# Fixed tiles with free lists, numbered admission, and a norm written in turned order, in a four-layer transformer kernel

## The chip, the cores and the metric

The kernel runs on one core of one Trainium2 chip. The metric is the device time of one execution in microseconds (us). Before the change, three runs gave a median of 2664.83 us (2660.78 to 2669.65).

The engines have short names in the profile: PE (TensorE, matrix products; PEld is its weight load), DVE (VectorE), ACT (ScalarE), POOL (GpSimd) and SP (SyncE, which here issues all DMAs).

## What is computed

Four transformer layers act in turn on x, of 16 samples x 256 tokens x 256 features, in fp32. Attention has 16 heads of 16 features. The context has 77 tokens a sample. Cut to what matters, for one sample:

```python
# layer 0: modulated by cond; self-attention masked by blocks, rotary on q and k
x = x + g_msa * (attn(rope(norm(x) @ Wq), rope(norm(x) @ Wk), norm(x) @ Wv, mask) @ Wo)
x = x + g_x   * (attn(norm(x) @ cq_W, ctx @ ck_W, ctx @ cv_W, mask_c) @ co_W)
x = x + g_mlp * (gelu(norm(x) @ W1 + b1) @ W2 + b2)
# layer 1: cross-attention alone; layer 2: self-attention, cross-attention, MLP
# layer 3: self-attention with rotary, cross-attention with rotary, MLP
```

Each norm subtracts the mean of a token's features, divides by their standard deviation, then scales and shifts by values that a small product of the condition gives ("modulation"). The attention inside is softmax(q k / 4) v.

## The kernel before

**Blocks and stages.** The unit of work is one sample in one sublayer, a *block* (256 tokens x 256 features, two tiles of 128 tokens). All of x stays in SBUF (`x_sb`). The sublayers are named by letters, which are also the ends of the tiles' names: a (self-attention, layer 0), ac (cross), b (MLP); cx (cross, layer 1); c (self, layer 2), cc (cross), d (MLP); e (self, layer 3), ec (cross), f (MLP). There are 16 blocks of each.

**One attention block**, in `attention` from line 726:

- `norm_tasks` (line 484): DVE takes mean and variance (`norm_stats`, 465), POOL makes the factor (`rstd_of`, 473) and writes the normed x into `xn` (line 497, two instructions of 128x256). For all but the first two blocks of stage a, DVE then turns 32x32 pieces of `xn` into `y` (line 526), SP sends `y` to DRAM (`yd`, line 532) and fetches it back with features on the partitions (`xr`, line 536), and ACT applies the modulation (`xT`, line 547). The two other blocks (`direct`) are turned by PE (line 505).
- PE makes q, k and v (lines 627, 679, 799). ACT and DVE write q and k into a tile `kq`, v goes to `vt`. With rotary, DVE and POOL rotate (lines 691, 694, 699) and PE turns back (719).
- Scores for the row maxima: PE in row tiles of 32 partitions (lines 840 and 852), DVE reduces each bank (lines 866, 870, 874) into `mx`. When all of a block's maxima are there, DVE turns `mx` (line 886), and SP moves them through DRAM into `kq` (lines 889, 893), where they enter the second product.
- Scores again, with the maximum subtracted (line 937), exponentials on ACT into `e` (949, 951), values on PE in column tiles (line 960), a turn, division and turn back on DVE and POOL (969, 976, 982, 986).
- `residual` (line 998): PE multiplies by the output weights (line 1007), DVE or POOL adds to x.

An MLP block makes `h` (PE line 1050, ACT line 1055) and ends in `residual` too.

**What sets the order.** All instructions are laid out by a planner in the kernel's own text, class `Order` (line 74). Each step is a task: an engine ("NO" for steps that only take a buffer), an assumed duration, its dependencies, buffers that it takes and holds, and a priority number, smaller first. `solve` simulates the engines on the host, and each engine's program is the order in which `solve` starts the tasks. On PE, ready tasks go by (priority, number). "NO", DVE, ACT and POOL go by the time at which a task became ready, then priority (lines 179 and 180). Tasks with `rp` 0 and 1 use different halves of PE's rows and are started in pairs (`choose`, line 154).

**Buffers.** `CAPS` (line 222) says how many there are of each kind: 8 PSUM banks "b", 5 "kq", 5 "v", 3 "mx", 2 "mr", 2 "ec" (four `e` tiles each), 1 "xn", 1 "y", 2 "ts" and so on. "b", "kq" and "v" come from free lists (`FREE`, line 82). All others are rings, made by rotating tile pools: a slot comes back only when all slots taken before it are back.

**Lines.** For "mx", "mr", "e" and "av" there is besides an order of places: a block joins the lines when it is admitted (`joins`, line 747), and a task with a `line` can start only when its block is at the head (`room`, line 119). The turn of the maxima (line 894) is in line "mr".

**Admission.** A block is admitted by a "NO" task (line 745), once its x is done, and takes a "kq" and a "v". Priorities are given out in steps of 10 in the order of the loops, which `wave` (line 1063) makes: for self- and cross-attention, it puts cross block b two steps after self block b. Some steps take theirs from this numbering: the load of x for block b (line 1186), and the third modulation "m0m" (line 1191), which waits for `admitted[-8]`, the eighth of the last blocks in that order.

Of the kernel before, what the change touches and what calls it, by code (L numbers as in the profile page):

```python
# [10 lines left out]
F32 = mybir.dt.float32  # L11
# [49 lines left out]
class Task:  # L61
    __slots__ = ("eng", "dur", "run", "deps", "take", "prio", "rp", "left", "ready", "outs", "held", "start", "end", "no", "since", "kind", "joins",
                 "line", "last", "more", "lat", "first", "mb")
# [10 lines left out]
class Order:  # L74
# [7 lines left out]
    FREE = ("b", "kq", "v")  # L82

# [3 lines left out]
    def add(self, eng, dur, run, deps=(), take=(), use=(), prio=0, rp=None, kind=None, joins=(),  # L87
            line=None, last=True, more=0.0, lat=0.0, first=False, mb=0.0):


        t = Task()
        t.joins, t.line, t.last, t.more, t.lat, t.first, t.mb = joins, line, last, more, lat, first, mb
# [11 lines left out]
    def solve(self):  # L104
        import heapq
        caps = self.caps
        taken = {k: 0 for k in caps}
        done_no = {k: set() for k in caps}
        ring = {k: 0 for k in caps}
        loose = {k: list(range(caps[k])) for k in self.FREE}  # L110
# [6 lines left out]
        lines = {}  # L117

        def room(t, more=()):
            if t.line is not None and (not lines.get(t.line[0]) or lines[t.line[0]][0] != t.line[1]):  # L120
                return False
            need = {}
            for h in list(t.take) + list(more):
                need[h.tag] = need.get(h.tag, 0) + 1
            return all(len(loose[k]) >= n if k in loose else taken[k] + n <= ring[k] + caps[k]
                       for k, n in need.items())

        def begin(ts):
# [6 lines left out]
            for t in ts:  # L135
                for h in t.take:
                    h.no = loose[h.tag].pop(0) if h.tag in loose else taken[h.tag]
                    taken[h.tag] += 1
                for name, key in t.joins:
                    lines.setdefault(name, []).append(key)  # L140
                if t.line is not None and t.last:
                    lines[t.line[0]].pop(0)
# [28 lines left out]
        while n_done < len(self.tasks):  # L171
            progress = True
            while progress:
                progress = False
                for eng in list(waiting):
# [3 lines left out]
                    cand.sort(key=lambda t: (t.prio, t.no) if eng == "PE" else (not t.first, t.prio, t.no) if eng == "SP" else  # L179
# [13 lines left out]
            while events and events[0][0] <= now + 1e-9:  # L193
                _, _, t = heapq.heappop(events)
                n_done += 1
                for h in t.held:
                    h.users -= 1
                    if not h.users and h.tag in loose:
                        loose[h.tag].append(h.no)
                    elif not h.users:  # L200
                        done_no[h.tag].add(h.no)
                        while ring[h.tag] in done_no[h.tag]:
                            done_no[h.tag].discard(ring[h.tag])
                            ring[h.tag] += 1
# [9 lines left out]
def pixart_kernel(ctx: ExitStack, tc: tile.TileContext, x, cond_t, ctx_in, mask_c, mask_s, tables, vecs, rows,  # L214
# [17 lines left out]
    kqs = [const.tile([P, 2, 2, 512], F32, name=f"kq{i}") for i in range(CAPS["kq"])]  # L232
    banks = [ps.tile([P, 512], F32, name=f"bank{i}") for i in range(CAPS["b"])]

# [42 lines left out]
    mrs, vs = [], []  # L277
# [5 lines left out]
    for j in range(CAPS["v"]):  # L283
        vs.append(const.tile([P, NT, H, 32], F32, name=f"vt{j}"))
# [54 lines left out]
    def load_weights(src, block, deps=(), prio=-1):  # L339

        if len(BLOCKS[block]) == 2:
            hs, views, tasks = [Hold("kq"), Hold("kq")], {}, {}

            def run(i, name, n):
                w = kqs[hs[i].no].rearrange("p a b n -> p (a b n)")
# [30 lines left out]
    def modulation(name, src, col, shift_at, scale_at, c_t, bias, norm=None, gate=None, deps=(), prio=0, gprio=None):  # L376
# [3 lines left out]
        def load():  # L380
            s["w"] = kqs[hw.no][:, 0]
# [29 lines left out]
        def load2():  # L411
            s["wg"] = kqs[hw2.no][:, 0]
# [11 lines left out]
        def rowtake():  # L424
            d = gate_d[g_row]
            pg, g2 = s["pg"], work.tile([P, NT, D], F32, tag="tmp", bufs=CAPS["tmp"], name=f"g2_{name}")
# [23 lines left out]
    def bias_tile(name, rest, deps, prio):  # L450
# [3 lines left out]
        def mm():  # L454
            s["p"] = psum(h)
            s["t"] = work.tile([P, 1, D], F32, tag="bias", bufs=CAPS["bias"], name=f"bias_{name}")
# [8 lines left out]
    def norm_stats(src, parts, n, name, c=""):  # L465
# [611 lines left out]
    def later(prio):  # L1077
        return prio + 1000
# [306 lines left out]
```

## Time and profile before

| | us |
|---|---|
| runs, median (lowest to highest) | 2664.83 (2660.78 to 2669.65) |
| the profiled execution's own time | 2664.59 |
| its span, first to last instruction | 2662.8 |
| time around the span | 1.8 |
| stage a with its start, about | 0 to 460 |
| ac / b / cx | 460 to 638 / 862 / 1122 |
| c / cc / d | 1122 to 1459 / 1633 / 1847 |
| e / ec / f | 1847 to 2249 / 2440 / 2663 |

The stage bounds are read from where the last results of one stage end (`oT`, `h`); neighbouring stages overlap there.

How to read the rows below. In a group of instructions, "L526 DVE STREAM_TRANSPOSE y_e<-xn_e ... x16 | 17.6, 1103 | 29.9 <-..." is: line, engine, operation, output and input, count, then the time that the group was busy (us), the mean of one (ns), the idle time of the engine just before, and who ended it. fp32 products appear as two records each. In a view by windows, each row has the window, its length, then busy time and count for PE, PEld, DVE, ACT and POOL, the granted clock of PE (1.00 is full), and the DMA share. In the view of a tile, a row has the shortest, median and longest duration in ns, then the first and last start in us. The profiled chain of work that ended last follows from the last instruction back to what released each step. PE's rows overlap in time, since a record's end is modelled; starts are measured.

### The profile page before, as it was taken

To read this page: it belongs to the slowest core of one execution; us is meant where nothing else is said; L and a number is where in the kernel's file an instruction comes from. 1 tells how busy PE (TensorE), PEld (TensorE's weight loads), DVE (VectorE), ACT (ScalarE), POOL (GpSimd) and SP (SyncE) were. 2 spreads that over 40 slices of the span, in tenths; PEclk is the share of its full clock that TensorE was granted. 3 is DMA by queue.
4 is the path that set the end of the run, shared out by engine and by line. 5 is a ranking of instruction groups with operands and counts; after the bars stand their busy time and mean duration, and the time that the engine had idled before them with its cause. 6 is when DMAs were issued, how large, how long until landed. Compare 5 with 4: busy or idle time off the path is not lost.

```text
span 2662.8 us, 55746 instructions
## 1 busy us (share of the span) xinstructions
PE 2595.9 (97%) x21512; PEld 1821.4 (68%) x21512; DVE 1678.8 (63%) x4537; ACT 1250.2 (47%) x2511; POOL 1062.0 (40%) x1413
## 2 busy tenths in 40 slices
PE   8999999999999899999999999999999999998999
PEld 5556565666888666566666667888666665666888
DVE  7888887774241677777776775211888887895110
ACT  2444445664333456555555564232455555554222
POOL 4233333556452364233334556432233334556310
PEclk9999999999999899999999999999999999998999
DMA  5101111234221121111111123211000001121110
GB/s 169 30 23 33 33 31 40 65 98 129 63 80 44 51 63 56 56 35 40 43 39 35 58 77 97 68 60 44 28 30 27 27 27 37 44 73 54 56 60 28
DMA packets 159747, 143.08 MB, mean 54 GB/s; under 512 B 24648, under 2 KB 124216, under 8 KB 158712
## 3 DMA queue, kind: packets, MB, share of 16 engines
q1 hardware_dynamic: 159480, 139.51, 16.9%
q8 instruction: 169, 2.77, 0.4%
q14 instruction: 98, 0.80, 0.1%
HBM read 91.86 MB, written 47.61 MB: 52 GB/s over the span
## 4 chain that ended last, share of the span: by engine, by line
PE 87%; DVE 6%; POOL 2%; ACT 2%; DMA 1%; issue 1%; DVEq 0%; ACTq 0%; SPq 0%; POOLq 0%
PE bank L1007 19%; PE bank L937 13%; PE bank L1050 12%; PE bank L960 11%; PE bank L627 7%; PE bank L840 7%; PE bank L679 6%; PE bank L799 5%; PE bank L852 2%; PE bank L719 2%; PE bank L930 2%; DVE mx_e L870 1%; DVE mx_c L870 0%; DVE mx_ec L874 0%; PE bank L390 0%
## 5 line engine op out<-in xcount | busy, mean ns | idle before, releaser
L937 PE MATMUL bank<-kq 32*128 32x256 f32 (+1 forms) x5120 | 615.8, 397 | 2.3 <-DMA kq<-mrow 0.8
L937 PEld LDWEIGHTS bank<-kq 32*128 32x128 f32 (+1 forms) x5120 | 350.2, 168 | 171.1 <-issue 99.0
L840 PE MATMUL bank<-kq 32*128 32x512 f32 x1536 | 420.5, 642 | 1.9 <-ACT e_e L951 1.6
L951 ACT ACTIVATE e_a<-bank 128x512 f32<-128x512 f32 x256 | 138.0, 596 | 178.7 <-PE bank L840 152.4
L866 DVE CUSTOM_DVE_ANT_0 junk<-bank,ctxT_masks 128x256 f32<-128x256 f32 x448 | 188.3, 420 | 36.5 <-issue 3.6
L951 ACT ACTIVATE e_e<-bank 128x512 f32<-128x512 f32 x256 | 136.1, 598 | 140.8 <-PE bank L840 79.3
L870 DVE TENSOR_REDUCE mx_c<-bank 128x2 f32<-128x512 f32 x256 | 160.2, 680 | 37.8 <-PE bank L840 36.9
L951 ACT ACTIVATE e_c<-bank 128x512 f32<-128x512 f32 x256 | 136.1, 599 | 97.2 <-PE bank L840 54.4
L870 DVE TENSOR_REDUCE mx_e<-bank 128x2 f32<-128x512 f32 x256 | 161.3, 680 | 25.3 <-PE bank L840 24.6
L852 PE MATMUL bank<-kq 32*128 32x154 f32 x2048 | 169.7, 312 | 4.2 <-ACT kq L634 3.0
L840 PEld LDWEIGHTS bank<-kq 32*128 32x128 f32 x1536 | 128.6, 185 | 34.8 <-issue 9.0
L852 PEld LDWEIGHTS bank<-kq 32*128 32x128 f32 x2048 | 132.3, 187 | 21.1 <-issue 4.6
L1013 DVE TENSOR_TENSOR x_sb<-x_sb,bank 128x512 f32<-128x512 f32 x80 | 54.0, 675 | 126.7 <-PE bank L1007 122.3
L1050 PE MATMUL bank<-xT_b,kq 128*128 128x256 f32 x512 | 117.1, 385 | 0.0
L1055 ACT ACTIVATE h_f<-bank,vec 128x256 f32<-128x256 f32 x128 | 52.3, 466 | 136.9 <-PE bank L1050 136.0
L1055 ACT ACTIVATE h_d<-bank,vec 128x256 f32<-128x256 f32 x128 | 52.0, 466 | 135.7 <-PE bank L1050 118.4
L1050 PE MATMUL bank<-xT_f,kq 128*128 128x256 f32 x512 | 113.5, 379 | 0.0
L1007 PE MATMUL bank<-kq,h_b 128*128 128x256 f32 x512 | 113.5, 379 | 0.0
L1050 PE MATMUL bank<-xT_d,kq 128*128 128x256 f32 x512 | 113.4, 380 | 0.0
L1007 PE MATMUL bank<-kq,h_f 128*128 128x256 f32 x512 | 113.1, 379 | 0.0
L1007 PE MATMUL bank<-kq,h_d 128*128 128x256 f32 x512 | 113.1, 379 | 0.0
L1050 PEld LDWEIGHTS bank<-xT_b,kq 128*128 128x128 f32 x512 | 97.8, 193 | 13.9 <-issue 0.8
(329 smaller groups left out, 5722.5 us busy)
## 6 DMA issues: line engine op xcount, KB each, us to landing
kq<-in_mod_dram SPq DMA_DIRECT2D x10, 512.0 KB
cin<-in_ctx_in_dram SPq DMA_DIRECT2D x36, 128.0 KB
x_sb<-in_x_dram SPq DMA_DIRECT2D x16, 256.0 KB
yd<-y_ac SPq DMA_DIRECT2D x16, 256.0 KB
xr_ac<-yd SPq DMA_DIRECT2D x16, 256.0 KB
yd<-y_b SPq DMA_DIRECT2D x16, 256.0 KB
xr_b<-yd SPq DMA_DIRECT2D x16, 256.0 KB
gb_b<-gate_g0m SPq DMA_DIRECT2D x16, 256.0 KB
```

Of the source, the lines that this page charges most:

```text
L627: nc.tensor.matmul(dst[:, g, :], lhsT=w[:, k, g * P:(g + 1) * P], rhs=xT[:, k, :], start=(k == 0), stop=(k == NC - 1))
L679: nc.tensor.matmul(u["p"][0:r, at:at + D], lhsT=xT()[:, k, t * P:t * P + r], rhs=w()[:, k, :], start=(k == 0), stop=(k == NC - 1))
L799: nc.tensor.matmul(ps[0:rows_n, t * D:(t + 1) * D], lhsT=xT[:, k, t * P:t * P + rows_n], rhs=wv[kv][:, k, :], start=(k == 0), stop=(k == N ...
L840: ls.append(lambda ps=ps, R=R, keys=keys: nc.tensor.matmul(ps.rearrange("p (s k) -> p s k", k=N), lhsT=s["qx"][R, 0, g, t * P:(t + 1) * P] ...
L852: ls.append(lambda ps=ps, R=R, keys=keys, tt=tt: nc.tensor.matmul(ps[:, 2 * tt * n:2 * (tt + 1) * n].rearrange("p (s k) -> p s k", k=n), l ...
L866: nc.vector.tensor_tensor_reduce(junk, u[i][:, i2 * N:(i2 + 1) * N], mb[:, t, :], -1.0, 3.0e38, ALU.add, ALU.min, m[:, i2, g, t:t + 1])
L870: nc.vector.tensor_reduce(m[:, :, g, t], u[i].rearrange("p (s k) -> p s k", k=N), AX.X, ALU.max, negate=True)
L937: (lambda ps=u[i], R=R, q=q: nc.tensor.matmul(ps[0:rows_n, q * N:(q + 1) * N], lhsT=s["kz"][R, q, g, kc * P:kc * P + rows_n], rhs=s["qx"][ ...
L951: nc.scalar.activation(e, u[i][0:rows_n], AF.Exp)
L960: nc.tensor.matmul(u5["p"][32 * r:32 * r + 32, 1 - q, :], lhsT=s["v"][0:rows_n, kc, 8 * g + 2 * r + 1 - q, :], rhs=s["e", g, kc, r][0:rows ...
L1007: nc.tensor.matmul(u["p"][:, t, :], lhsT=lhsT(k, t), rhs=w()[:, k, :], start=(k == 0), stop=(k == nk - 1))
L1050: nc.tensor.matmul(u["p"][:, j, :], lhsT=wv["w1"][:, k, f * P:(f + 1) * P], rhs=s["xT"][:, k, :], start=(k == 0), stop=(k == NC - 1))
```

## The change

1. All SBUF buffers are made once as fixed tiles (`SHAPES`, `pools`), and `buf(hold)` gives the tile whose number the planner drew. All kinds now have free lists: a slot is back as soon as its own users are done. The counts in `CAPS` stay. The four `e` tiles of one "ec" become slices of one tile. The DRAM buffers `yd` and `mrow` go by the drawn number too.
2. `joins`, `line` and the lines are gone. The two value products of a group of heads (line 960) may run in either order; the first to run starts the sum in PSUM.
3. "NO" tasks go by priority instead of by the time at which they became ready. `wave` sorts the blocks by b plus 0, 16 or 32 for the first, second and third kind of block.
4. The norm on POOL (line 497), except in the two direct blocks, writes `xn` with the features of each half in the order (f, j) instead of (j, f): it reads x in order and writes every 32nd element. The turn on DVE (line 526) then reads runs of 32 neighbours instead of every fourth element. The planner's duration for that turn goes from 0.7 to 0.75.

The diff, cut to its core (each `work.tile` or `small.tile` elsewhere becomes `buf` of its hold in the same way):

```diff
@@ solve
-        taken = {k: 0 for k in caps}
-        done_no = {k: set() for k in caps}
-        ring = {k: 0 for k in caps}
-        loose = {k: list(range(caps[k])) for k in self.FREE}
+        loose = {k: list(range(n)) for k, n in caps.items()}
...
         def room(t, more=()):
-            if t.line is not None and (not lines.get(t.line[0]) or lines[t.line[0]][0] != t.line[1]):
-                return False
             need = {}
             for h in list(t.take) + list(more):
-                need[h.tag] = need.get(h.tag, 0) + 1
-            return all(len(loose[k]) >= n if k in loose else taken[k] + n <= ring[k] + caps[k]
-                       for k, n in need.items())
+                if h.no < 0:
+                    need[h.tag] = need.get(h.tag, 0) + 1
+            return all(len(loose[k]) >= n for k, n in need.items())
...
-                    cand.sort(key=lambda t: (t.prio, t.no) if eng == "PE" else (not t.first, t.prio, t.no) if eng == "SP" else
+                    cand.sort(key=lambda t: (t.prio, t.no) if eng == "PE" else (not t.first, t.prio, t.no) if eng in ("SP", "NO") else
                               (not t.first, t.ready - self.FAVOUR * any(h.tag == "b" for h in t.held), t.prio, t.no))
...
-                    if not h.users and h.tag in loose:
+                    if not h.users:
                         loose[h.tag].append(h.no)
-                    elif not h.users:
-                        done_no[h.tag].add(h.no)
-                        while ring[h.tag] in done_no[h.tag]:
-                            done_no[h.tag].discard(ring[h.tag])
-                            ring[h.tag] += 1
@@ norm_tasks
         def scale():
-            xn = s["xn"] = work.tile([P, NT, D], F32, tag="xn", bufs=CAPS["xn"], name=f"xn_{name}")
+            xn = s["xn"] = buf(hn)
             for t in range(NT):
-                nc.gpsimd.tensor_scalar(xn[:, t, :], x_sb[:, b, t, :], s["mv"][:, t, 0:1], s["rstd"][:, t:t + 1],
-                                        ALU.subtract, ALU.mult)
+                to, of = xn[:, t, :], x_sb[:, b, t, :]
+                if not direct:
+                    to, of = (a.rearrange(f"p (c {z}) -> p c j f", c=NC, f=4) for a, z in ((to, "f j"), (of, "j f")))
+                nc.gpsimd.tensor_scalar(to, of, s["mv"][:, t, 0:1], s["rstd"][:, t:t + 1], ALU.subtract, ALU.mult)
...
         def turn32():
-            s["y"] = work.tile([P, 4, NT * NC * 32], F32, tag="y", bufs=CAPS["y"], name=f"y_{name}")
+            s["y"] = buf(hy)
             nc.vector.transpose(s["y"].rearrange("p f (u i) -> p f u i", i=32),
-                                s["xn"].rearrange("p t (c j f) -> p f (t c) j", j=32, f=4))
+                                s["xn"].rearrange("p t (c f j) -> p f (t c) j", j=32, f=4))
@@ attention
         x_t = add("NO", 0.0, admit, deps=[x_done[b], *norm_deps],
-                  take=[h_kq, h_v], prio=prio,
-                  joins=[("mx", nm), ("mr", nm)] +
-                        [(i, (nm, g, kc)) for i in ("e", "av") for g in range(NC) for kc in range(nk)])
+                  take=[h_kq, h_v], prio=prio)
...
-        a = add("DVE", 0.2, turn, first=True, deps=red, take=[h_mr], use=[h_mx], prio=prio, line=("mr", nm))
+        a = add("DVE", 0.2, turn, first=True, deps=red, take=[h_mr], use=[h_mx], prio=prio)
@@ wave
-    def wave(kinds):
-
-        nxt = [0] * len(kinds)
-        order = []
-        step = 0
-        while any(i < B for i in nxt):
-            for j in range(len(kinds) - 1, -1, -1):
-                b = step - 2 * j
-                if 0 <= b < B:
-                    order.append((j, b))
-                    nxt[j] += 1
-            step += 1
-        return order
+    def wave(*late):
+
+        return sorted(((j, b) for j in range(len(late)) for b in range(B)), key=lambda z: (z[1] + late[z[0]], -z[0]))
@@ the loops
-    for j, b in wave([0, 1]):
+    for j, b in wave(0, 16):
...
-    for j, b in wave([0, 1, 2]):
+    for j, b in wave(0, 16, 32):
...
-    for j, b in wave([0, 1]):
+    for j, b in wave(0, 16):
```

## The prediction

> **What bounds the kernel now.** I read the page first: busy time by engine, and under it the chain that ended last.
>
> ```profile
> span 2662.8 us, 55746 instructions
> PE 2595.9 (97%) x21512; PEld 1821.4 (68%) x21512; DVE 1678.8 (63%) x4537; ACT 1250.2 (47%) x2511; POOL 1062.0 (40%) x1413
> PE 87%; DVE 6%; POOL 2%; ACT 2%; DMA 1%; issue 1%; DVEq 0%; ACTq 0%; SPq 0%; POOLq 0%
> ```
>
> PE is the bound. All its idle time is 2662.8 - 2595.9 = 66.9 us, so a change that only reorders can win no more than that, plus what it takes out of PE's busy time. The timeline of PE in a self-attention stage shows what could be taken out:
>
> ```profile
> 2055.16 0.48 PE L937 MATMUL bank<-kq 32*128 32x256 f32 x2
> ...
> 2055.92 0.38 PE L937 MATMUL bank<-kq 32*128 32x256 f32 x2
> 2056.24 1.99 PE L1007 MATMUL bank<-w_e,oT_e 128*128 128x256 f32 x8
> 2058.16 1.07 PE L960 MATMUL bank<-e_e,vt 128*32 128x256 f32 x16
> ```
>
> Where PE stays in one shape, in the MLP stages, 32 records of 128x256 take 6.91 us (the chain in order of time), 0.216 each. Here eight of them run from 2056.24 to 2058.16, 1.92 us instead of 1.73. The pair of row-tiled tasks ahead of them runs 1.08 us (2055.16 to 2056.24) where its four rounds need 0.86. So each change of tile shape costs about 0.2 us, and the order of the tasks on PE sets how many changes there are. That is the only large lever here.
>
> Then the busy times by stretch of time (us, PE, PEld, DVE, ACT, POOL). First three steady stretches, of stages a, c and e; then the four handovers between attention stages, and the end of stage ec.
>
> ```profile
> 100.00:400.00 300.00, 299.21 (x2817) 178.01 (x2812) 260.73 (x1029) 142.53 (x269) 99.65 (x129) 1.00 0.11 31
> 1150.00:1400.00 250.00, 249.85 (x2265) 156.04 (x2264) 185.71 (x380) 144.87 (x281) 85.22 (x115) 1.00 0.14 41
> 1900.00:2200.00 300.00, 297.33 (x2695) 185.79 (x2696) 251.87 (x530) 151.76 (x289) 95.57 (x132) 0.99 0.09 28
> ```
>
> ```profile
> 425.00:475.00 50.00, 47.25 (x534) 30.55 (x526) 29.56 (x88) 30.16 (x57) 21.73 (x34) 1.00 0.21 62
> 1090.00:1125.00 35.00, 32.58 (x289) 18.54 (x288) 27.81 (x63) 16.05 (x36) 12.71 (x19) 0.95 0.24 66
> 1405.00:1470.00 65.00, 61.40 (x678) 39.09 (x674) 38.77 (x107) 40.35 (x84) 34.78 (x48) 1.00 0.14 42
> 2215.00:2270.00 55.00, 50.24 (x520) 30.87 (x514) 36.40 (x115) 30.53 (x60) 25.58 (x37) 1.00 0.11 35
> 2395.00:2440.00 45.00, 37.21 (x317) 23.18 (x313) 32.58 (x93) 17.95 (x34) 39.20 (x57) 0.81 0.20 69
> ```
>
> In steady state PE is full in all three stretches, with DVE at 87%, 74% and 84%. The idle time sits at the handovers: 2.75 + 2.42 + 3.60 + 4.76 = 13.5 us.
>
> **The order of the stages does not move.** The text of the loops suggests that self- and cross-attention blocks were interleaved and now run one after the other. The trace says that they already run one after the other. The maxima of stage a and of its cross-attention ac are turned (line 886) at these times:
>
> ```profile
> L886 DVE STREAM_TRANSPOSE mt_a<-mx_a x16: 211/211/213, 50.8 to 432.2; 128x32 f32<-128x32 f32 x16
> L886 DVE STREAM_TRANSPOSE mt_ac<-mx_ac x16: 171/211/213, 432.3 to 610.5; 128x32 f32<-128x32 f32 x16
> L874 DVE TENSOR_REDUCE mx_ac<-bank x32: 429/468/480, 388.7 to 454.9; 128x4 f32<-128x308 f32 x32
> ```
>
> Admission went by readiness, all a blocks are ready early, and an ac block only when its a block is done. So the new keys (b, then 16 + b, then 32 + b) give the order that the trace has: I cost that edit at nothing in steady state. What does change is who comes first on PE at a handover. Before, the first ac blocks have smaller priority numbers than the last a blocks. The last row shows the result: the maxima of the first ac blocks start at 388.7, yet the first of their turns is at 432.3, 0.1 us after the last turn of a. They did their work early, and then stood in line "mr". Now the last a blocks go first, and nobody stands in line.
>
> **Part by part.**
>
> (1) Fixed tiles, free lists, no lines. No instruction and no DMA is added or removed, none moves to another engine. No buffer count changes. In steady state blocks pass first-in first-out anyway, so rings and lists give the same slots. I cost it at 0 there. At the handovers it can win at most the 13.5 us of PE idle; at least 0. Nearest row for what cannot be won is the drain at the end of ec, where no next block exists: 45.0 - 37.2 = 7.8 us idle. I take half, 6.8 us.
>
> (2) Steps that the new numbers move. Modulation "m0m" waits for the eighth of the last admissions, now ac block 8 instead of 11. It issues a 512 KB and a 256 KB load on SP, takes a kq buffer for each, and 16 records on PE (2.2 us where the trace has one at 873.40). The PE work is due either way; on SP it passes the row-maxima transfers of three blocks at most, and those are put first. Cover: four other kq buffers with blocks in flight. Without it, one admission would slip by one load. The loads of x for blocks 3 on also get smaller numbers and pass ten context loads on SP, which stage ac needs only from 388 us. I take 0 for both.
>
> (3) The turn on DVE (line 526) reads 16 bytes apart before, and contiguous runs of 32 after. Groups by line, mean ns after the comma:
>
> ```profile
> L526 DVE STREAM_TRANSPOSE y_e<-xn_e 128x512 f32<-128x512 f32 x16 | 17.6, 1103 | 29.9 <-DMA yd<-y_e 9.4 <-POOL x_sb L563 9.0 <-DMA yd<-y_d 9.0
> L969 DVE STREAM_TRANSPOSE ts_e<-bank 128x512 f32<-128x512 f32 x32 | 22.6, 707 | 14.1 <-PE bank L960 13.9
> L497 POOL TENSOR_SCALAR xn_e<-x_sb,mv_e,rstd_e 128x256 f32<-128x256 f32 x32 | 38.9, 1223 | 3.7 <-DVE y_e L526 1.9 <-DVE y_d L526 0.8
> L982 POOL TENSOR_TENSOR od_e<-ts_e,rec_e 128x128 f32<-128x128 f32 x64 | 24.4, 401 | 99.5 <-DVE rec_e L976 99.5
> L699 POOL TENSOR_TENSOR qk_e<-qk_e,r_qk_e 128x512 f32<-128x512 f32 x32 | 40.5, 1269 | 81.8 <-DVE r_qk_e L694 78.5 <-PE bank L719 3.4
> ```
>
> Same operation, same size, contiguous source: 0.71 us against 1.10. That source is PSUM; the turn of half the size from SBUF to SBUF (line 986, mean 429 ns) lies on the same line, so SBUF is no slower. Ends: 1.10 (no gain) and 0.70; I take 0.71. There are 10 x 16 - 2 = 158 such turns (two blocks go by PE), so DVE loses 158 x 0.39 = 61.6 us of work. How much reaches the end? DVE is 6% of the chain, 160 us of its 1679 busy: about 9.5% of DVE's time is on the path. 61.6 x 0.095 = 5.9 us. From below: 0. From above: all of it in the self stages a and e, where DVE is at 84 to 87%: (14 + 16) x 0.39 = 11.7 us. I take 5.9. In the MLP stages it is worth nothing, PE runs without a change of shape there. What is late next is PE itself.
>
> (4) The norm write on GpSimd (line 497): 316 of its 320 instructions (those of the two blocks by PE stay) now write elements 128 bytes apart, and read as before. No row has such a write. Nearest: line 982 writes runs of 16 and takes 3.1 ns an element (401/128); line 699 writes contiguously and takes 2.5 (1269/512), some of the difference being a fixed part. The norm itself takes 4.8 (1223/256). A gain is excluded, since reads are contiguous in both and writes get less so. [...] line 526 against 969 is 1.10/0.71 = 1.55. Applied to GpSimd, 1.22 becomes 1.90, 316 x 0.68 = 215 us more of its time, 40% busy becomes 48%, and with 2% of the chain (53 of 1062 us, 5%) that is +10.7 us. By the rows it is 0: even the slow turn moves an element in 1103/512 = 2.2 ns, and GpSimd spends 4.8 on each, so a write that takes that long is hidden behind its own work. I take 0 and keep +10.7 for the range.
>
> **The sum.** The profiled execution took 2664.59 us (span 2662.8 and 1.8 around it), 0.24 under the median of 2664.83. 2664.59 - 6.8 - 5.9 = 2651.9, so 2652 us, -0.5%. Against the median it is the same to the digit that matters. A difference under 0.3% (8 us, 2656.8 to 2672.8) can't be told from no change here.
>
> **The rivals.**
>
> *A, the forecast*, 2652; its own range 2639 (13.5 and 11.7 both won) to 2657. Chance 0.43.
>
> *B, it does nothing*: DVE's saved time lands in its own idle (37% of the span), and the handovers stay as they are because DMA latency and the last block's chain set them, not places. For it: the only long wait of PE that isn't the start, 7.8 us on xT_cx (line 627), is a norm chain that no part shortens by more than 0.4 us. 2660 to 2665. Chance 0.24.
>
> *C, slower by more changes of shape*. Priorities decide which task PE takes next. If the new order strings row-tiled pairs singly between other work, each extra run costs 1.08 - 0.86 = 0.21 us. One more in each of the 16 x 7 = 112 attention blocks is 23.5 us: 2664.6 - 5.9 + 23.5 = 2682. It outweighs the gains and shows as slower from about (8 + 5.9)/0.21 = 66 extra runs. For it: nothing in the planner's choice among ready tasks favours the shape that PE is in. Against: in steady state the order of readiness and place is the same. Chance 0.18, with a little from (4).
>
> *D, the same lever the other way*: as many runs fewer, as free buffers let two pairs follow each other. 2651.9 - 23.5 = 2628. For it: the cross blocks' maxima that stood in line for 40 us held mx buffers. Against: eight PSUM banks hold only two pairs. Chance 0.15.
>
> **How the numbers follow.** Faster by over 0.3%: A's 0.43 and D's 0.15, less a piece of A near the bound: 0.57. Slower: C, 0.18. Same: the rest, 0.25. The range reaches to D and to C, 2622 to 2682, which leaves out some 6% below and 8 to 10% above.
>
> **What would show it.** Line 526 at 0.71 us, x158, and DVE's busy time at 1679 - 62 = 1617 (step 3). Line 497 at 1.22 us; at 1.6 or more [...] step 4 is wrong. The first turn of ac within some 10 us of its eighth reduction, and PE idle of 7 us instead of 13.5 over the four handovers (step 1). PE busy within 10 us of 2596: A and B; 2615 or more is C, 2575 or less is D. The forecast is wrong above all if the new numbers change how PE's tasks fall together in steady state, which the trace of before can't show.

## The result, and the profile after

The changed kernel takes 2630.61 us (median of four runs, 2626.68 to 2638.0), the kernel before 2667.24 us in the same comparison (2660.78 to 2672.21). The ratio is 0.9867 (95% interval 0.9835 to 0.9899): 1.3% faster, where 0.5% was forecast. The time lies inside the range and near the figure of rival D (2628), but not by D's mechanism, as shown below.

The page's first lines for the changed kernel, and its two groups that part 4 touches (line 497 is now 491, line 526 is 519):

```profile
span 2629.7 us, 56144 instructions
PE 2575.5 (98%) x21512; PEld 1813.2 (69%) x21512; DVE 1627.7 (62%) x4537; ACT 1255.4 (48%) x2511; POOL 1113.5 (42%) x1413
...
L491 POOL TENSOR_SCALAR xn<-x_sb,mv,rstd 128x256 f32<-128x256 f32 x320 | 451.1, 1464 | 108.4 <-DVE y L519 97.8
...
L519 DVE STREAM_TRANSPOSE y<-xn 128x512 f32<-128x512 f32 x158 | 110.9, 702 | 298.9 <-DMA yd<-y 257.6
```

The same instructions do the same work (x21512, x4537, x2511, x1413); the 398 more in the first line are all semaphore waits of the sequencers. The turn went from 1.10 to 0.70 us; the norm write from 1.22 to 1.46. PE's idle time went from 66.9 to 2629.7 - 2575.5 = 54.2 us, and its busy time fell by 20.4 us.

The turns of the maxima (line 886, now 872) in the view of a line, which gives no letter of a stage any more because the tiles are shared:

```profile
L872 DVE STREAM_TRANSPOSE mr<-mx x112: 211/211/215, 51.5 to 2384.4; 128x32 f32<-128x32 f32 x112
```

From the single starts behind this row: 15th and 16th turn of stage a at 392.0 and 414.5, first turn of ac at 426.1, 1.3 us after that block's last reduction ended at 424.8. Before, that reduction ended at 394.1 and the turn came at 432.3, after 38 us in line. Most of this wait is gone because the reductions of ac now start later (414.6 instead of 388.7); the turn itself comes only 6 us earlier. The stages come in the same sequence as before.

The windows show where PE's idle time went. First the four handovers, placed at the same work as before's; then stage ec, and its last 45 us. Columns are as before: length, then PE, PEld, DVE, ACT, POOL.

```profile
422.80:472.80 50.00, 49.00 (x584) 30.77 (x580) 27.98 (x77) 30.17 (x55) 20.49 (x28) 1.00 0.17 51
1069.00:1104.00 35.00, 34.48 (x245) 23.28 (x246) 29.54 (x64) 15.40 (x32) 14.02 (x21) 1.00 0.18 56
1393.60:1458.60 65.00, 64.62 (x738) 43.07 (x735) 46.77 (x124) 41.64 (x87) 34.80 (x48) 1.00 0.17 51
2194.50:2249.50 55.00, 53.67 (x599) 35.88 (x591) 40.13 (x124) 33.82 (x66) 26.09 (x38) 1.00 0.13 39
2228.30:2414.60 186.30, 179.89 (x1810) 120.47 (x1809) 153.80 (x484) 100.56 (x197) 124.29 (x175) 0.99 0.20 64
2369.60:2414.60 45.00, 40.30 (x377) 27.97 (x370) 32.38 (x102) 23.96 (x47) 41.33 (x56) 0.96 0.26 85
```

The handovers have 1.00 + 0.52 + 0.38 + 1.33 = 3.2 us of PE idle, against 13.5. Stage ec has 186.3 - 179.9 = 6.4. The row of before for stage ec, which the prediction did not show:

```profile
2248.80:2440.00 191.20, 176.89 (x1767) 116.04 (x1768) 157.80 (x473) 95.90 (x186) 117.88 (x172) 0.96 0.19 59
```

That is 14.3 us idle and a mean clock of 0.96. The clock is a third place to look. In both traces the granted clock is either 1.00 or 0.50. Below are the longest stretches at 0.50, and the sum over all of them: before, and then after.

```profile
875.00:888.70 13.70, 5.91 (x21) 5.05 (x21) 9.28 (x12) 2.36 (x4) 10.90 (x8) 0.50 0.16 53
...
2397.30:2414.40 17.10, 12.66 (x80) 8.60 (x84) 14.04 (x38) 2.50 (x4) 14.04 (x19) 0.50 0.23 70
sum 51.20, PE 38.83 PEld 24.71 DVE 39.05 ACT 11.13 POOL 38.99; mean PE 6.47 PEld 4.12 DVE 6.51 ACT 1.86 POOL 6.50
```

```profile
876.70:886.90 10.20, 3.46 (x8) 2.84 (x9) 8.21 (x12) 1.09 (x2) 8.64 (x7) 0.50 0.16 52
...
2385.40:2388.80 3.40, 3.14 (x7) 2.01 (x7) 2.78 (x11) 1.95 (x4) 2.54 (x2) 0.50 0.26 90
sum 23.80, PE 16.80 PEld 13.00 DVE 16.39 ACT 5.61 POOL 18.64; mean PE 3.36 PEld 2.60 DVE 3.28 ACT 1.12 POOL 3.73
```

At half clock PE does about half as much. In the trace of the changed kernel, eight products of one shape take 3.61 us from their first start to the next row's start in the stretch 1607.1 to 1610.5, and 1.72 us just after it, at full clock:

```profile
1607.10 3.68 PE L992 MATMUL bank<-w_c,oT 128*128 128x256 f32 x8 [1.73 <-DVE oT L971]
1610.71 1.07 PE L945 MATMUL bank<-ec,v 77*32 77x256 f32 x16
...
1622.18 1.89 PE L992 MATMUL bank<-w_c,oT 128*128 128x256 f32 x8
1623.90 7.07 PE L992 MATMUL bank<-kq,ec 128*128 128x256 f32 x32
```

Over all neighbouring products of that shape, the median from start to start is 216 ns at 1.00 and 427 ns at 0.50, in both traces.

PE was busy for 38.8 us at half clock before, and for 16.8 after. If half of that is lost, the loss went from 19.4 to 8.4 us. So the span of 33.1 us less splits, in these two profiles, into 12.7 of idle, about 11.0 of clock (an estimate), and a rest of 9.4 in PE's busy time. That rest may be waiting inside what counts as busy, since the ends of PE's records are modelled; no view here shows it.

### The profile page after: what moved, and what is told of

It is laid out like the page before. It is cut to its first block, busy times and chain, and to the rows that moved or that the text cites. A ratio compares the mean times of both kernels' runs of the same rounds, so it can differ in the third digit from the quotient of the medians.

```text
span 2629.7 us, 56144 instructions
## 1 busy us (share of the span) xinstructions
PE 2575.5 (98%) x21512; PEld 1813.2 (69%) x21512; DVE 1627.7 (62%) x4537; ACT 1255.4 (48%) x2511; POOL 1113.5 (42%) x1413
## 5 line engine op out<-in xcount | busy, mean ns | idle before, releaser
L936 ACT ACTIVATE ec<-bank 128x512 f32<-128x512 f32 (+1 forms) x1152 | 608.5, 596 | 514.0 <-PE bank L828 260.7
L491 POOL TENSOR_SCALAR xn<-x_sb,mv,rstd 128x256 f32<-128x256 f32 x320 | 451.1, 1464 | 108.4 <-DVE y L519 97.8
L858 DVE TENSOR_REDUCE mx<-bank 128x2 f32<-128x512 f32 x544 | 341.6, 681 | 46.0 <-PE bank L828 43.7
L945 PE MATMUL bank<-ec,v 128*32 128x256 f32 (+1 forms) x5120 | 347.9, 385 | 5.8 <-ACT ec L936 3.6
L1035 PE MATMUL bank<-xT,kq 128*128 128x256 f32 x1536 | 341.4, 379 | 0.0
L992 PE MATMUL bank<-kq,ec 128*128 128x256 f32 x1536 | 339.7, 379 | 0.0
L992 PEld LDWEIGHTS bank<-kq,ec 128*128 128x128 f32 x1536 | 291.5, 190 | 39.5
L1035 PEld LDWEIGHTS bank<-xT,kq 128*128 128x128 f32 x1536 | 290.5, 190 | 40.4 <-issue 1.6
L862 DVE TENSOR_REDUCE mx<-bank 128x4 f32<-128x308 f32 x512 | 211.9, 468 | 55.4 <-PE bank L922 25.3
L854 DVE CUSTOM_DVE_ANT_0 junk<-bank,ctx 128x256 f32<-128x256 f32 x448 | 188.8, 421 | 45.2 <-PE bank L828 12.2
```

The costliest lines, as they stand in the source:

```text
L491: nc.gpsimd.tensor_scalar(to, of, s["mv"][:, t, 0:1], s["rstd"][:, t:t + 1], ALU.subtract, ALU.mult)
L854: nc.vector.tensor_tensor_reduce(junk, u[i][:, i2 * N:(i2 + 1) * N], mb[:, t, :], -1.0, 3.0e38, ALU.add, ALU.min, m[:, i2, g, t:t + 1])
L858: nc.vector.tensor_reduce(m[:, :, g, t], u[i].rearrange("p (s k) -> p s k", k=N), AX.X, ALU.max, negate=True)
L862: nc.vector.tensor_reduce(m[:, :, g].rearrange("p s t -> p t s"), u[i][:, 0:4 * n].rearrange("p (t s k) -> p t s k", s=2, k=n), AX.X, ALU. ...
L936: nc.scalar.activation(e, u[i][0:rows_n], AF.Exp)
L945: nc.tensor.matmul(u5["p"][32 * r:32 * r + 32, 1 - q, :], lhsT=s["v"][0:rows_n, kc, 8 * g + 2 * r + 1 - q, :], rhs=s["e", g, kc, r][0:rows ...
```

## The price of the half clock, from all runs

Each timed run gives its span and its mean granted clock. Since the clock is 1.00 or 0.50, the time at half clock is 2 x (1 - clock) x span, to some 5 us (the clock has three digits). Over 199 runs of the kernels below, each taken against the mean of its own kernel and batch of runs, a microsecond at half clock goes with 0.38 us more span (correlation 0.92). By the 216 and 427 ns above, about 0.5 would be the price if PE never idled in it (an estimate). So two executions of one kernel differ mostly by this term. With it taken out, kernels can be compared "at equal clock": that is an estimate (the last column), since the price was found between runs of one kernel and is carried over to differences between kernels. It is also a correlation; no run separates a price of the clock from late waits that bring both.

| kernel (runs) | ratio to before, 95% | mean span | half clock | span less 0.383 x half clock |
|---|---|---|---|---|
| before (43 / 24 / 12, by batch) | 1 | 2663.4 / 2662.4 / 2662.3 | 51.3 / 51.5 / 51.9 | 2643.8 / 2642.7 / 2642.4 |
| changed (4) | 0.9867 (0.9835 to 0.9899) | 2629.7 | 25.0 | 2620.1 |
| turn_only (22) | 0.9979 (0.9969 to 0.9989) | 2658.2 | 49.3 | 2639.3 |
| no_turn (6) | 0.9908 (0.9885 to 0.9931) | 2639.3 | 43.1 | 2622.8 |
| numbers_only (22) | 0.9999 (0.9987 to 1.0011) | 2662.7 | 64.2 | 2638.1 |
| lines_kept (6) | 0.9928 (0.9910 to 0.9946) | 2644.6 | 35.3 | 2631.1 |
| lists_only (11) | 1.0053 (1.0036 to 1.0069) | 2677.0 | 55.5 | 2655.7 |
| old_numbers (5) | 1.0416 (1.0394 to 1.0437) | 2776.3 | 156.6 | 2716.2 |
| before_lag15 (14) | 1.0009 (0.9997 to 1.0021) | 2665.6 | 52.6 | 2645.5 |
| after_lag15 (6) | 0.9891 (0.9872 to 0.9911) | 2636.4 | 31.6 | 2624.3 |
| ot_first (6) | 0.9937 (0.9918 to 0.9956) | 2644.2 | 32.6 | 2631.7 |
| lines_ot3 (7) | 0.9944 (0.9925 to 0.9964) | 2646.8 | 34.8 | 2633.5 |
| before_ot3 (6) | 0.9922 (0.9904 to 0.9939) | 2640.1 | 48.4 | 2621.6 |
| after_ot3_told (5) | 0.9866 (0.9844 to 0.9887) | 2625.6 | 58.8 | 2603.0 |

For the change itself the runs say what the two profiles said: about 26 us less at half clock, worth some 10 us by this estimate, and 23 us that remain at equal clock.

## The experiments

The theory after the result: most of the gain comes from the order (parts 1 to 3), a small part from the turn (part 4). The rivals: the turn alone; the numbers alone; luck of a greedy planner, in which any small edit could have moved the time as much.

**The turn alone, and all but the turn.** *turn_only* is the kernel before with only part 4 (without the planner's figure for it, so that the order stays):

```diff
-                nc.gpsimd.tensor_scalar(xn[:, t, :], x_sb[:, b, t, :], s["mv"][:, t, 0:1], s["rstd"][:, t:t + 1],
-                                        ALU.subtract, ALU.mult)
+                to, of = xn[:, t, :], x_sb[:, b, t, :]
+                if not direct:
+                    to, of = (a.rearrange(f"p (c {z}) -> p c j f", c=NC, f=4) for a, z in ((to, "f j"), (of, "j f")))
+                nc.gpsimd.tensor_scalar(to, of, s["mv"][:, t, 0:1], s["rstd"][:, t:t + 1], ALU.subtract, ALU.mult)
...
-                                s["xn"].rearrange("p t (c j f) -> p f (t c) j", j=32, f=4))
+                                s["xn"].rearrange("p t (c f j) -> p f (t c) j", j=32, f=4))
```

*no_turn* is the changed kernel with just this edit undone.

> The kernel before with part 4 alone: GpSimd writes the norm in turned order, DVE turns contiguous runs. Planner and its figures untouched, so every engine has the order of before. Theory T (the turn): if DVE's time is what PE waited for, this alone gives a third or more of the 33 us, 2645 to 2655. Theory O (the order): the turn is worth little, 2658 to 2666; line 526 falls to 0.71 us, line 497 stands at 1.46 as in the changed kernel, which shows that the price is the write's and not the order's.

> The changed kernel with part 4 undone: norm written in the order of x, DVE turn reading 16 bytes apart. The planner's figures stay, so every engine has the order of the changed kernel. Theory O: within 6 us of the changed kernel, 2630 to 2637. Theory T: 2645 or more. Line 497's place goes back to 1.22 us and the turn to 1.10.

Alone, part 4 wins 0.21%, 2665.25 to 2660.69: 4.6 us between the medians, 5.6 by the ratio. Its own row in the groups by line of *turn_only* has the new price of the norm write, with the order of before:

```profile
L500 POOL TENSOR_SCALAR xn_c<-x_sb,mv_c,rstd_c 128x256 f32<-128x256 f32 x32 | 45.0, 1461 | 0.2
```

and in *no_turn*, with the new order and the old write, it is back:

```profile
L488 POOL TENSOR_SCALAR xn<-x_sb,mv,rstd 128x256 f32<-128x256 f32 x320 | 392.0, 1233 | 127.6 <-DVE y L517 115.7 <-DVE rec L959 3.7
```

So the 1.46 us are the write's and not the order's. Without the turn the changed kernel still wins 0.92%, some 25 us. In the new order the turn seems worth 10 us (2640.49 against 2630.61), more than expected; the intervals of the two ratios just overlap (from 0.9885 to 0.9899), so the size is uncertain. The order is the same in both kernels; the table puts 7 of the 10 us down to the clock (43 us at half clock against 25), and 3 remain at equal clock.

**The numbers alone; the lists alone; the lists with the old numbers.** *numbers_only* is before with only part 3 (NO by priority, the sorted `wave`; only the main lines of its edit are shown). *lists_only* is the changed kernel with parts 3 and 4 undone. *old_numbers* is the changed kernel with only the old `wave` put back. In the two latter, every step that opens `e` also needs the block's `oT`, which is the edit of *ot_first* below; so they are not single changes against the changed kernel. Against *ot_first*, *old_numbers* is one.

```diff
-                    cand.sort(key=lambda t: (t.prio, t.no) if eng == "PE" else (not t.first, t.prio, t.no) if eng == "SP" else
+                    cand.sort(key=lambda t: (t.prio, t.no) if eng == "PE" else (not t.first, t.prio, t.no) if eng in ("SP", "NO") else
...
-    for j, b in wave([0, 1]):
+    for j, b in wave(0, 16):
```

> The kernel before with part 3 alone: takers of buffers by priority, blocks numbered b, 16 + b, 32 + b; rings, lines and the old norm stay. Theory O with its place at the handovers: about half of the gain, 2640 to 2655, with PE idle at the handovers lower. If free lists and lines do all of it: 2660 to 2668.

> The changed kernel with parts 3 and 4 undone: fixed tiles, free lists and no lines, but the numbering, the sort by readiness and the norm of before. (The output tile oT is taken by whichever step of a block comes first.) Numbers alone gave nothing and lines put back cost 15 us, so either free lists and missing lines give the gain by themselves, 2640 to 2650, or they need the new numbers, because without lines only the numbers hold the older block in front: then 2660 or more.

> The changed kernel with the loops' numbering of before (cross block b two steps after self block b), while buffers still go by priority and without lines. (oT as in lists_only.) If admission by place makes no difference to the order of the stages, as the prediction said of the change as a whole: within 15 us of 2631. If place now decides, self and cross blocks really interleave, and PE sees another mix: 2680 or more, or a gain if the mix balances DVE.

The numbers alone change nothing: 0.9999, where half the gain was expected. Yet the idle time at the four handovers fell in that kernel from 13.5 to 6.1 us, as the sum over its windows there shows:

```profile
sum 205.00, PE 198.91 PEld 129.91 DVE 146.27 ACT 115.58 POOL 87.88; mean PE 49.73 PEld 32.48 DVE 36.57 ACT 28.89 POOL 21.97
```

By the table it is 5 us better at equal clock and stands 13 us longer at half clock, which gives the 5 back. The lists alone (parts 1 and 2, with the rule on `oT`) are slower by 0.5%. The old numbers with admission by place cost 132 us against *ot_first* and are 4% slower than before: the reductions of ac (128x308) begin at 138.7 us in its trace while those of a run on to 610.5, so self- and cross-attention blocks were then really interleaved, and half-clock time tripled. So the sorted numbers are no gain by themselves; they keep the sequence that readiness used to give, once place decides.

**The lines.** *lines_kept* is the changed kernel with the lines "mx", "mr" and "e" put back ("av" stays out; the code that serves the lines comes back too and is not shown):

```diff
-                  take=[h_kq, h_v], prio=prio)
+                  take=[h_kq, h_v], prio=prio, joins=[("mx", nm), ("mr", nm)] + [("e", (nm, g, kc)) for g in range(NC) for kc in range(nk)])
...
-        t_mx = add("NO", 0.0, open_mx, deps=[q_t, k_t], take=[h_mx], prio=prio)
+        t_mx = add("NO", 0.0, open_mx, deps=[q_t, k_t], take=[h_mx], prio=prio, line=("mx", nm))
...
-        a = add("DVE", 0.2, turn, first=True, deps=red, take=[h_mr], use=[h_mx], prio=prio)
+        a = add("DVE", 0.2, turn, first=True, deps=red, take=[h_mr], use=[h_mx], prio=prio, line=("mr", nm))
...
-                          prio=prio)
+                          prio=prio, line=("e", (nm, g, kc)))
```

> The changed kernel with the lines mx, mr and e put back (a block gets its place at admission), all else as changed: free lists, numbers, turn. If the lines held work back, 2640 to 2652, slower than the changed kernel by 10 us or more. If rings or numbers did it all, 2627 to 2635.

It loses 15 us of the gain (2646.05 against 2630.61). But it is still 19 us under the kernel before, so the lines are not all of it: the turn makes up 5 to 10 of these, and the other 9 to 14 belong to free lists, numbers and the missing line "av" together, which no run divides further. Its handovers have 5.0 us of idle, little more than the 3.2 without lines. Its stage ec, in the view by windows, is what went back:

```profile
2232.20:2427.70 195.50, 181.35 (x1806) 119.70 (x1801) 153.80 (x480) 98.82 (x195) 120.35 (x169) 0.98 0.18 58
```

That is 14.2 us idle, as before the change (14.3).

**Luck.** The planner assumes a pause of 0.13 us between engines. *before_lag15* and *after_lag15* set it to 0.15 in each kernel, an edit without any purpose:

```diff
-    LAG = 0.13
+    LAG = 0.15
```

> The kernel before with one figure of the planner changed: the pause that it assumes between engines, 0.15 in place of 0.13 us. Nothing is added or taken away; the order of the tasks falls otherwise. Theory L (luck): the time moves by 10 us or more either way, as much as parts of the change. Theory O: within 6 us of 2665.

> The changed kernel with the planner's pause between engines at 0.15 in place of 0.13 us. Theory L: moves by 10 us or more, and could come near the kernel before. Theory O: within 6 us of 2631, and 25 us or more under before_lag15.

The kernel before moves little (1.0009). The changed one gets 8 us slower by the medians; the intervals of its ratios (0.9872 to 0.9911, and 0.9835 to 0.9899) overlap, so part of the 8 may be scatter. The distance between the two stays (2667.89 to 2638.22, 29.7 us). So the gain as a whole does not hang on this figure. One such edit for each kernel was made, so 8 us is a rough size only; differences below it between single plans are not put down to a cause here.

**What line "e" held up.** The first step that opens `e` for a block takes one of two `oT` tiles. With the line, every later such step stands behind it, those of other blocks too. *ot_first* is the changed kernel, without any line, in which each of these steps needs the block's `oT`. *lines_ot3* is *lines_kept* with three `oT` tiles, and *before_ot3* is the kernel before with three, and nothing else:

```diff
-                    if g == 0 and kc == 0:
-                        s["oT"] = buf(h_ot)
+                    s["oT"] = buf(h_ot)
...
-                t_e = add("NO", 0.0, open_e, deps=[qx_t, v_t, barrier], take=[h_e] if g or kc else [h_e, h_ot],
+                t_e = add("NO", 0.0, open_e, deps=[qx_t, v_t, barrier], take=[h_e, h_ot],
```

```diff
-            "ts": 2, "oT": 2, "rope": 2, "qk": 4, "tmp": 2, "gb": 3, "wa": 1, "ctx": 2,
+            "ts": 2, "oT": 3, "rope": 2, "qk": 4, "tmp": 2, "gb": 3, "wa": 1, "ctx": 2,
```

> The changed kernel with one rule more and no lines: every step that opens an e buffer of a block needs that block's oT buffer, not the first step alone. Theory W (what the lines did): the line e made all of a block's exponentials wait behind its first, and that one waits for one of two oT buffers; without the line the later ones pass it. Then this rule alone brings back the loss of lines_kept, 2641 to 2651. Rival: the lines kept blocks apart from each other, and this does nothing: 2627 to 2635.

> The kernel before with three oT buffers instead of two, nothing else of the change. Theory W: the oT buffers were what was short, and most of the order's part of the gain comes without the change, 2640 to 2652. If free lists and numbers are what counts: 2655 to 2668.

> lines_kept with three oT buffers instead of two, nothing else. Theory W: no block waits for an oT, the lines cost nothing, and 2646 falls to 2630 to 2642, with PE idle in stage ec at 7 us instead of 14. Rival (the lines themselves): stays at 2643 to 2649.

*ot_first* comes to 2645.85, the same as *lines_kept* (2646.05). So a wait for `oT` alone, without any line, is enough for what the lines cost. *before_ot3* speaks for it from the other side: one number, and the kernel before takes 2641.54, a ratio of 0.9922. At equal clock this one number does as much as the whole change (2621.6 against 2620.1). The page of that kernel, and its stage ec:

```profile
span 2637.5 us, 55758 instructions
...
PE 2583.4 (98%) x21512; PEld 1820.0 (69%) x21512; DVE 1681.5 (64%) x4537; ACT 1247.1 (47%) x2511; POOL 1062.3 (40%) x1413
```

```profile
2238.00:2428.00 190.00, 186.17 (x1821) 126.42 (x1820) 159.93 (x480) 100.34 (x196) 120.92 (x175) 1.00 0.20 63
```

PE's idle time is 54.1 us, as in the changed kernel (54.2). In stage ec it fell from 14.3 to 3.8. The last layer, from its first product to the end, takes 800.5 us of the profile instead of 818.3 (changed kernel: 799.7). Where it got shorter is seen at the last exponentials of stage ec, which the MLP behind them waits for. The rows are of the kernel before, of the changed kernel from 2380 us on, and of *before_ot3*:

```profile
L951 ACT ACTIVATE e_ec<-bank x128: 573/592/637, 2238.7 to 2432.5; 77x512 f32<-77x512 f32 x128
L936 ACT ACTIVATE ec<-bank x16: 583/594/623, 2385.3 to 2399.4; 77x512 f32<-77x512 f32 x16
L951 ACT ACTIVATE e_ec<-bank x128: 572/592/626, 2228.6 to 2406.7; 77x512 f32<-77x512 f32 x128
```

From the last exponential to the end of the span all three take 230 to 231 us. From the layer's first product (at 1844.5, 1830.0 and 1837.0) to that exponential they take 588.0, 569.4 and 569.7. So all that the last layer gains, it gains ahead of that barrier. *lines_kept* takes 584.0 there and *ot_first* 580.7.

*before_ot3* also shows what the line "mr" was worth. The first ac block still stands in it, from its reductions at 387.8 to its turn at 431.4:

```profile
L874 DVE TENSOR_REDUCE mx_ac<-bank x32: 433/469/481, 387.8 to 454.0; 128x4 f32<-128x308 f32 x32
L886 DVE STREAM_TRANSPOSE mt_ac<-mx_ac x4: 169/198/211, 431.4 to 454.5; 128x32 f32<-128x32 f32 x4
```

Yet that kernel wins 21 us, and its four handovers idle 5.3 us.

*lines_ot3* missed: 2630 to 2642 was expected and 2647.26 measured. Its last layer did get shorter, 808.6 against 814.3 in *lines_kept* (changed kernel: 799.7), with 9.8 us of idle in ec, but all that lies ahead of the last layer took 17 us longer. About 9 of these 17 go with the clock: the execution in the trace was the slowest of the seven (2658.70), and it stood 47.8 us at half clock ahead of the last layer, *lines_kept* 23.9. The other 8 us are no more than an edit without any purpose moved the changed kernel. So the third tile won back some 6 of the 14.6 us in the last layer and nothing in the whole: the theory is borne out in part at most.

**Both together.** *after_ot3_told* is the changed kernel with three `oT` tiles, and with the planner's duration for the pair of norm writes set to what the trace has, 2 x 1.46:

```diff
-            "ts": 2, "oT": 2, "rope": 2, "qk": 4, "tmp": 2, "gb": 3, "wa": 1, "ctx": 2,
+            "ts": 2, "oT": 3, "rope": 2, "qk": 4, "tmp": 2, "gb": 3, "wa": 1, "ctx": 2,
...
-        t3 = add("POOL", 2.5, scale, deps=[t2], take=[hn], use=[hs], prio=prio)
+        t3 = add("POOL", 2.95, scale, deps=[t2], take=[hn], use=[hs], prio=prio)
```

> A version that the runs point to: the changed kernel with three oT buffers, and the planner told what the norm write takes now (2.95 in place of 2.5 us for the pair). Theory W and a planner that knows its figures: 2615 to 2628. If the changed kernel's order was already free of the oT wait, and its figures matter little: 2628 to 2640.

2626.58, ratio 0.9866: within the intervals the same as the changed kernel. PE idles only 41.7 us in its profile, the least of all, and at equal clock it would be 17 us ahead (2603.0 against 2620.1). But it stands 59 us at half clock instead of 25, which takes back 13. Which of its two edits does what was not tested.

## Why the prediction was right, and where it was off

The direction was right, and the range held. The size was not: 12.7 us were forecast and 33 to 37 measured, outside the likeliest case's own range (2639 to 2657). That the range held is in part luck: its lower end was set for D, whose mechanism did not occur. The steps below bear the numbers of the prediction's parts.

*Step 3, the turn.* Right. 0.702 us measured for 0.71, 5.6 us won alone for 5.9. That SBUF is no slower as a source held too: the turn of this size from PSUM (line 969, now 954) takes 0.707 us in the same trace. DVE's busy time went to 1627.7 where 1617 was the mark: the turns themselves fell by 158 x (1.104 - 0.702) = 63.5 us, and DVE's other rows took some 12 more.

*Step 4, the norm write.* Between the two ends. 1.46 us, that is 20% more, where 0 was taken from the rows, and 55% for the range: the ratio of DVE's two turns (1.10 to 0.71), carried over to GpSimd's write. Both were the author's estimates. What was taken as hidden behind GpSimd's own work shows as 0.24 us more, and no run shows that the ratio of a read on DVE holds for a write on GpSimd. By the way of the working it would cost 316 x 0.24 = 76 us of POOL's time, and 5% of that is 4 us; it is contained in the 5.6 us that part 4 wins as a whole.

*Step 1, the handovers: a right mark, and a wrong price.* 6.8 us was taken and 10.3 disappeared, the first turn of ac came 1.8 us after its reduction. But *numbers_only* has 7.4 of these us without any gain; by the estimate of the table the time came back as half clock. With the lines in place (*lines_kept*) the handovers idle 5.0 us. The wait in line "mr" was real, but it was not what the time hung on: *before_ot3* keeps it and has 5.3.

*Step 1, steady state and drain: the step that failed.* "In steady state blocks pass first-in first-out anyway, so rings and lists give the same slots. I cost it at 0 there," and the drain of stage ec was taken as "what cannot be won". Line "e" was not asked about: it put all exponentials of later blocks behind a wait for one of two `oT` tiles. Without it, stage ec idles 6.4 us instead of 14.3, and its last 45 us run at clock 0.96 instead of 0.81. The barrier on all exponentials of ec is passed 19 us earlier, counted from the start of the layer, and from there to the end nothing changed. *ot_first* and *before_ot3* price the wait for `oT` at 15 to 21 us. That the line brought it about in just this way is the reading that fits these two; *lines_ot3* does not confirm it. The same step also put rings against lists at nothing; what the lists do with the new numbers, at most 9 to 14 us, was not measured alone. A look at which buffer each step in line "e" takes, and at the 14.3 us of idle over the whole of stage ec rather than over its last 45 us, might have led there.

*The missing term.* The sum had no term for the clock, although before's row for the end of ec shows 0.81. By the estimate above it is worth 10 us of the result.

*The rivals.* A (idle time and the turn) gave the direction, about a third of the size, and not the place. B's point against A held in part: the 8-us wait at the start of stage cx is still there (8.0 us on `xT`, line 619, in the waits of the changed kernel). D's time came by another way: counted over the trace in order of starts, with rows and columns of a product rounded up to 32, 64 or 128, PE changes its tile shape 1375 times after and 1351 times before, 24 more. Counted by exact sizes it is 2317 against 2341, 24 fewer. Either way that is far from the 112 fewer of D. PE's busy time of 2575.5, which was to be D's sign, did not tell of shapes: half clock lengthens records too (those of 128x256 in a tile of 128x128 have a median of 379 ns at full clock and 634 at half, in both traces), and PE's 22 us less of busy time at half clock are worth some 11 of the 20.4 by which it fell (an estimate). C did not happen; 24 changes at the 0.2 us that the prediction estimated from two places of the trace would be 5 us.

*The order of the stages.* It did not move, as claimed. That the edit costs nothing by itself was too simple: *old_numbers* shows that with admission by place the old numbers cost 132 us (against *ot_first*).

**Open.** Why *lines_ot3* loses ahead of the last layer what it wins there. What won the 14.5 us that the changed kernel gains ahead of the last layer (its start moved from 1844.5 to 1830.0; three `oT` tiles alone moved it by 7.5). Why one plan draws 25 us at half clock and another 59, with less idle time: in the traces of before and of the changed kernel all 11 stretches follow gaps of PE, but no single gap was taken out to test it. And whether the 21 us of *before_ot3* would stand under other small edits: it was tried with one plan only.

## What to carry to other kernels

Before a rewrite of a scheduler, look for the step ahead of a barrier whose buffer has the smallest count, and for what stands in line behind it: here one more tile of a kind gave 0.8% on the kernel before, against 1.3% for the whole change. (In the changed kernel, with one figure of the planner set right besides, it gave nothing that shows in the time.) Idle time of the bounding engine had no fixed price here (*numbers_only* idles 7.4 us less at the handovers, at a ratio of 0.9999): take the granted clock into the sum, and check in the runs whether a gain in idle time is given back there. And edit a figure without meaning in a greedy plan first: if that moves the time by some 8 us, as it may have here, parts of a change that differ by less have not been told apart.

## What the runs showed of the hardware

- In all 14 profiles the granted clock was 1.00 or 0.50 and nothing between, at 0.50 in stretches of 3.4, 6.8, 10.2, 13.7, 17.1 and 20.5 us, multiples of 3.4 (97 stretches; three more, of 1.0 to 1.8 us, end with the program). In the traces of before and of the changed kernel, all 11 follow 3.4 us in which PE idled for 7.6% to 64.5%. That much idle time was not enough by itself: of the stretches of 3.4 us at full clock, counted in steps from the first one at half, 111 have 7% or more of PE idle, and 11 of them went before half clock. Nor did 3.4 us of busy PE always bring back the full clock: in *lines_ot3* PE was busy through all of 13.7 us, by its records, and the clock stayed at half.

```profile
916.20:929.90 13.70, 13.70 (x90) 9.90 (x93) 6.75 (x21) 3.95 (x8) 5.78 (x7) 0.50 0.14 44
```

  What sets the clock is not in the profile, so why it stays down is open.
- A microsecond at half clock went with 0.38 us more span over 199 runs, and this explains most of the scatter between runs of one kernel (correlation 0.92).
- GpSimd writes fp32 elements 128 bytes apart 20% slower than neighbours (1.46 us in the changed kernel against 1.22 before, for 128x256). DVE's turn reads 16 bytes apart 57% slower than runs of 32 (1.104 us in *no_turn* against 0.702 in the changed kernel, for 128x512).
